# A fixed order of instructions, opposite phases of two batch halves and a shorter state update in an attention-GRU recurrence

## The chip, the cores and the metric

The kernel runs on one core of one Trainium2 chip. The metric is device time in microseconds (us) of one execution, the median of several. The profile of a run is the hardware profiler's record of one of these executions; the profile of the kernel before that the prediction was read from is of a further one. All numbers below are of that core, and all times that are compared are of runs in the fast state. (e14 and e15 ran once each, so their state is unknown; of them only the traces are compared, step by step.)

The runs fell on several chips, and this turned out to matter. The kernel before takes 2136 to 2138 us on chips 2 and 13, and 2112 to 2113 us on chips 3 and 14. I call the first kind *late* and the second *steady*, for a reason that the experiments show. Every run was timed beside runs of the kernel before on its own chip.

## The reference, cut to what matters

1024 users with 100 history items of 128 numbers go through a GRU. Its states are the keys of an attention, and also the inputs of a second recurrence, AUGRU, whose state at each user's own last step feeds a small prediction network:

```python
def augru_step(h, inp):
    x_t, a_t = inp                                   # key, attention weight of the step
    ti = jnp.concatenate([h, x_t], axis=-1)
    r = jax.nn.sigmoid(ti @ aug_Wr.T + aug_br)
    u = jax.nn.sigmoid(ti @ aug_Wu.T + aug_bu)
    h_hat = jnp.tanh(jnp.concatenate([h * r, x_t], axis=-1) @ aug_Wh.T + aug_bh)
    u = a_t[:, None] * u
    h_new = (1.0 - u) * h + u * h_hat
    return (h_new, h_new)
# ... 100 steps, state 128 wide, float32
comb = jnp.concatenate([user, item, hist_sum, item * hist_sum, attention_feature], axis=1)
scores = mlp(comb, 3 layers, sigmoid)[:, 0]          # "prediction"
```

## The kernel before

The kernel does GRU, attention and AUGRU one after the other; the GRU part is the same before and after. For AUGRU the users are sorted by length, so that a step needs only the columns of users that are still alive: a half (512 users) starts 512 columns wide and shrinks to 96. State and gates are tiles of 128 partitions by that width. Each gate is two matmuls into one PSUM bank: one on the key, which *opens* it, and one on the state, which *closes* it.

```python
ps = tile_pool(name="ps3", bufs=6, space=PSUM)      # gates
pa = tile_pool(name="pa3", bufs=2, space=PSUM)      # all else, tag "a"
...
def load_key(t, i):                                  # key of step t, half i
    k = wp.tile([P, HB], F32, name="k3", bufs=6)
    if q < WHOLE:                                    # steps 0 to 7: TensorE transposes
        ...
    else:                                            # later: VectorE, in blocks of 32
        nc.vector.transpose(k..., r[:, :w, ts(n, R)])

def step(t, i):
    ...
    pr = gate(wr, h, "pr")
    nc.scalar.activation(pr, pr, AF.Sigmoid, bias=later["br"])
    nc.vector.tensor_mul(r, h, pr)
    pu = gate(wu, h, "pu")
    nc.scalar.activation(pu, pu, AF.Sigmoid, bias=later["bu"])
    nc.vector.tensor_mul(u, pu, at)
    later["pace"] = u[:, 0:1]
    ph = gate(wh, r, "ph")
    nc.scalar.activation(ph, ph, AF.Tanh, bias=later["bh"])
    nc.vector.tensor_sub(ph, ph, h)
    nc.vector.tensor_mul(ph, u, ph)
    nc.vector.tensor_add(h, h, ph)

def predict(g, i):                                   # 128 users whose last step is past
    gather(part, part_d, g, i)                       # indirect DMA, issued by GpSimd
    ...                                              # 14 matmul passes, 4 sigmoids
    nc.gpsimd.indirect_dma_start(out=out..., in_=y)

for t in range(T):                                   # rows of keys: gathered ahead,
    for i in range(NH):                              # in blocks of 8 steps, by GpSimd
        load_att(t + 2, i)
        step(t, i)
        ... next(ahead, None)                        # some row gathers of the next block
        load_key(t + 1, i)
    for g in range(GH):
        if left <= g * P < widths[t]:
            for i in range(NH):
                predict(g, i)
```

In AUGRU the order on TensorE and ScalarE is written only for the preparations up to step 1; in the steps a scheduler orders the instructions of every engine. The row gathers are paced: each waits for a one-column copy of a fresh update weight.

## Time and profile before

| | before |
|---|---|
| median time, three runs | 2137.28 us (2135.11 to 2139.23) |
| span of the profiled execution | 2109.6 us |
| time of that execution itself | 2111.61 us |
| TensorE busy, whole span | 97% |
| AUGRU steps 2 to 99 in the profile | 604.9 us |

A page gives busy time of each engine, then 40 slices of the span in tenths, then the granted TensorE clock in tenths. A timeline line has start, length, engine, source line, operation, written and read tiles, and in brackets how long the engine had idled and what ended it. "PEld" is TensorE's weight load. The lines that carry the argument stand in the prediction.

One row of the table deserved more attention than I gave it: the profiled execution was 25.7 us faster than the median of the timed ones.

### The profile page before, as it was taken

How to read it: one execution, taken by the hardware profiler on the slowest of the kernel's cores; microseconds unless marked ns; L12 is line 12 of the kernel's file. 1: busy time of each engine (PE TensorE's matmuls, PEld its weight loads, DVE VectorE, ACT ScalarE, POOL GpSimd, SP SyncE). 2: the span in 40 equal slices, each digit the busy share in tenths (PEclk: the TensorE clock that was granted, in tenths of full speed). 3: DMA queues.
4: the chain of work that ended last, by engine and by line, in shares of the span. 5: the costliest groups of instructions: out<-in, count | busy, mean ns of one | idle time of the engine just before them, and what ended most of it. 6: DMA issues, size and time to landing. Idle time of an engine off the chain costs nothing. (4 is left out here: it accounts for less than half of the span.)

```text
span 2109.6 us, 26501 instructions
## 1 busy us (share of the span) xinstructions
PE 2046.8 (97%) x8260; PEld 979.0 (46%) x8260; DVE 1767.4 (84%) x3025; ACT 827.9 (39%) x1510; POOL 1293.4 (61%) x1295
## 2 busy tenths in 40 slices
PE   8999999999999999999999999996999999999987
PEld 3343333333333333333333333333444555688886
DVE  6888999989989888989898888996677777888765
ACT  3334343433334343334333434332443444454444
POOL 0234939479887969595969494996733443343321
PEclk9999999999999999999999999998999999999998
DMA  4533233333323343333423332213633333333221
GB/s 118 113 92 101 87 101 109 109 95 96 96 88 93 113 121 110 94 109 109 141 87 100 101 101 87 91 46 87 190 88 90 108 99 90 95 96 88 75 56 26
DMA packets 253553, 205.58 MB, mean 97 GB/s; under 512 B 74790, under 2 KB 215818, under 8 KB 253402
## 3 DMA queue, kind: packets, MB, share of 16 engines
q1 hardware_dynamic: 241082, 171.36, 29.2%
q0 software_dynamic: 12320, 32.44, 5.3%
q8 instruction: 67, 1.10, 0.2%
q14 instruction: 84, 0.69, 0.1%
HBM read 147.68 MB, written 54.40 MB: 96 GB/s over the span
## 5 line engine op out<-in xcount | busy, mean ns | idle before, releaser
L483 PE MATMUL ps<-x,wih 128*128 128x512 f32 x1200 | 591.7, 602 | 4.2 <-DMA x<-in_hist_x 4.2
L483 PE MATMUL ps<-hn,whh 128*128 128x512 f32 x1188 | 574.4, 592 | 0.0
L483 PEld LDWEIGHTS ps<-x,wih 128*128 128x128 f32 x1200 | 220.6, 190 | 327.1 <-issue 254.3
L483 PEld LDWEIGHTS ps<-hn,whh 128*128 128x128 f32 x1188 | 225.7, 190 | 284.1 <-issue 275.5
L469 POOL TENSOR_TENSOR xm<-x,m 128x512 f32<-128x512 f32 x200 | 244.8, 1224 | 128.9 <-DMA m<-mask_d 128.6
L514 ACT ACTIVATE ps<-ps,bih 128x512 f32<-128x512 f32 x200 | 132.4, 662 | 473.9 <-DVE ps L513 473.9
L495 ACT ACTIVATE r<-ps,brz 128x512 f32<-128x512 f32 x200 | 137.4, 687 | 391.3 <-PE ps L483 390.3
L470 POOL TENSOR_TENSOR hist<-hist,xm 128x512 f32<-128x512 f32 x200 | 265.9, 1330 | 15.7
L573 POOL TENSOR_TENSOR pooled<-pooled,kw 128x512 f32<-128x512 f32 x190 | 255.7, 1346 | 14.9
L572 POOL TENSOR_TENSOR kw<-kt,e 128x512 f32<-128x512 f32 x190 | 220.3, 1159 | 64.1 <-DVE e L728 64.0
L157 POOL DMA_INDIRECT rows<-keys_d,idx_k x208 | 200.0, 961 | 78.8 <-POOL rows L156 48.3
L552 DVE TENSOR_TENSOR kq<-hn,item 128x512 f32<-128x512 f32 x200 | 228.1, 1179 | 0.0
L631 PE MATMUL pm<-hn,wk 128*32 128x512 f32 x1200 | 214.1, 600 | 6.2 <-DVE f L665 3.7
L631 PE MATMUL pm<-kq,wkq 128*32 128x512 f32 x1200 | 210.9, 594 | 0.0
L631 PE MATMUL pm<-mv,w 128*32 128x512 f32 (+1 forms) x808 | 198.8, 603 | 1.4 <-ACT mv L670 0.9
L156 POOL COPY rows<-u 128x1 f32<-128x1 f32 x202 | 32.4, 181 | 259.1 <-DVE u L972 258.3
L665 DVE TENSOR_TENSOR f<-pm,q 128x512 f32<-128x512 f32 x200 | 128.3, 683 | 54.3 <-PE pm L631 54.2
L518 DVE TENSOR_TENSOR d<-hn,ps 128x512 f32<-128x512 f32 x198 | 136.0, 687 | 34.9 <-ACT ps L514 32.6
L519 DVE TENSOR_TENSOR d<-ps,d 128x512 f32<-128x512 f32 x200 | 138.3, 692 | 23.8 <-ACT ps L515 7.2
L513 DVE TENSOR_TENSOR ps<-ps,u 128x512 f32<-128x512 f32 x200 | 140.0, 700 | 21.6 <-PE ps L483 0.5
L503 DVE SCALAR_TENSOR_TENSOR u<-ps,bhh,r 128x512 f32<-128x512 f32 x198 | 146.9, 742 | 13.2 <-PE ps L483 12.9
L967 ACT ACTIVATE pr<-pr,br 128x96 f32<-128x96 f32 (+42 forms) x198 | 91.6, 463 | 136.5 <-PE pr L962 133.7
(163 smaller groups left out, 2969.9 us busy)
## 6 DMA issues: line engine op xcount, KB each, us to landing
x<-in_hist_x SPq DMA_DIRECT2D x212, 256.0 KB
keys_d<-kt SPq DMA_DIRECT2D x46, 1024.0 KB
m<-mask_d SPq DMA_DIRECT2D x200, 128.0 KB
keys_d<-kt SPq DMA_DIRECT2D x64, 64.0 KB
rows<-keys_d,idx_k POOLq DMA_INDIRECT x208, 2.8
s_b<-mv SPq DMA_DIRECT2D x200, 8.0 KB
mask_i<-in_mask SPq DMA_DIRECT2D x8, 200.0 KB
at<-att_d SPq DMA_DIRECT2D x32, 48.0 KB
```

Of the source, the lines that this page charges most:

```text
L157: nc.gpsimd.indirect_dma_start(out=r[:, k, :], out_offset=None, in_=keys_d[q], in_offset=bass.IndirectOffsetOnAxis(ap=idx_k[:, k, i : i + ...
L469: nc.gpsimd.tensor_mul(d, x, m)
L470: nc.gpsimd.tensor_add(acc, acc, d)
L483: nc.tensor.matmul(p, lhsT=w[:, g, :], rhs=v, start=(j == 0), stop=(j == len(parts) - 1),)
L495: nc.scalar.activation(r, pr, AF.Sigmoid, bias=brz[:, 0:1])
L503: nc.vector.scalar_tensor_tensor(out=u, in0=ph, scalar=bhh[:, 2:3], in1=r, op0=ALU.add, op1=ALU.mult,)
L513: nc.vector.tensor_add(pi, pi, u)
L519: nc.vector.tensor_mul(d, pz, d)
L552: nc.vector.tensor_mul(kq, h, item[:, self.cols])
L572: eng.tensor_mul(d, k, w)
L573: eng.tensor_add(acc, acc, d)
L631: nc.tensor.matmul(p[i][s, :], lhsT=w[:, s], rhs=v, start=start, stop=stop)
```

## The change

The intent: every AUGRU instruction stands in a written order on every engine, in which half 0 and half 1 work in opposite phase, so that TensorE closes a gate of one half while the other half is on ScalarE and VectorE. The state update h + u(c - h) becomes uc - (u - 1)h with (u - 1)h computed ahead of the tanh. Gates get a ring of seven banks, all else gets one. The prediction is cut into pieces that are issued one per half-step. The preparations before step 2 are reordered as well (the attention weights are gathered before the first keys are transposed), and a half-step opens the candidate (`ph`) before the update gate (`pu`).

```diff
-        ps = pools.enter_context(tc.tile_pool(name="ps3", bufs=6, space=PSUM))
-        pa = pools.enter_context(tc.tile_pool(name="pa3", bufs=2, space=PSUM))
+        ps = pools.enter_context(tc.tile_pool(name="ps3", bufs=7, space=PSUM))
+        pa = pools.enter_context(tc.tile_pool(name="pa3", bufs=1, space=PSUM))
 ...  (sort_weights, half 1 between the instructions of half 0's step 1)
             first = pa.tile([P, HB], F32, tag="a", name="first")
 ...
-        def step(t, i):
 ...  (shown above)
+        def half_step(t, i):
+            w, h = widths[t], h3[i][:, : widths[t]]
+            before, after = ((t - 1, 1), (t, 1)) if i == 0 else ((t, 0), (t + 1, 0))
+            if before in resets:
+                open_state(*before)                  # closes ph of the other half, tanh
+            pr = close_gate(t, i, "pr", wr, h)
+            pu = close_gate(t, i, "pu", wu, h)
+            nc.scalar.activation(pr, pr, AF.Sigmoid, bias=later["br"])
+            nc.scalar.activation(pu, pu, AF.Sigmoid, bias=later["bu"])
+            state = states.pop(1 - i, None)
+            if state is not None:
+                nc.vector.tensor_mul(state[0], state[0], state[1])       # u c
+            r = wp.tile([P, HB], F32, name="r3")[:, :w]
+            nc.vector.tensor_mul(r, h, pr)
+            if state is not None:
+                nc.vector.tensor_sub(state[3], state[0], state[2])       # h of the other half
+            if t == 1 and i == 0:
+                sort_weights(1, sorted_rows[1], gates[1])
+            nc.vector.tensor_mul(pu, pu, att.pop((t, i))[:, :w])
+            rest = wp.tile([P, HB], F32, name="rest")[:, :w]
+            nc.vector.scalar_tensor_tensor(                              # (u - 1) h
+                out=rest, in0=pu, scalar=1.0, in1=h, op0=ALU.subtract, op1=ALU.mult
+            )
+            later["pace"] = rest[:, 0:1]
+            resets[t, i] = r, pu, rest
+            if after[0] < T and (*after, "pr") not in opened:
+                open_gates(*after)
+            if t + 2 < T:
+                load_att(t + 2, i)
+            if t + 1 < T:
+                load_key(t + 1, i)
 ...
-        def predict(g, i):
+        def predict(g, i, pool, tag):
             gather(part, part_d, g, i)
+            yield
 ...  (a yield after each group of matmuls and of activations)
         def spread(q):
+            ahead = 2 if widths[FIRST[q]] > HB // 2 else 3
-            slots = NH * ((FIRST[q] - FIRST[q - 1] if q > 2 else FIRST[q]) - 2)
+            slots = NH * (FIRST[q] - (FIRST[q - 1] if q > 2 else 1) - ahead)
 ...
             for i in range(NH):
+                half_step(t, i)
                 for _ in range(due.pop(0) if due else 0):
                     next(ahead, None)                # row gathers
+                if jobs:
+                    try:
+                        next(jobs[0])                # one piece of a prediction
+                    except StopIteration:
+                        jobs.pop(0)
+            for g in range(1, GH):
                 if left <= g * P < widths[t]:
+                    jobs += [predict(g, i, pa, "a") for i in range(NH)]
 ...
-        with ExitStack() as pools:
+        with ExitStack() as pools, tc.manual_schedule():
             augru_phase(pools, widths)
```

More of the change, by code (lines that the diff above doesn't have):

```diff
@@ L879, in augru_phase, with bank @@
         kp = pools.enter_context(tc.tile_pool(name="kp3", bufs=4))
-        ps = pools.enter_context(tc.tile_pool(name="ps3", bufs=6, space=PSUM))
-        pa = pools.enter_context(tc.tile_pool(name="pa3", bufs=2, space=PSUM))
+        ps = pools.enter_context(tc.tile_pool(name="ps3", bufs=7, space=PSUM))
+        pa = pools.enter_context(tc.tile_pool(name="pa3", bufs=1, space=PSUM))
         wr, wu, wh = later["wr"], later["wu"], later["wh"]
-        keys, att, opened = {}, {}, {}
+        keys, att, opened, resets, states = {}, {}, {}, {}, {}
         later["pace"] = None
+        def bank(name):
+            return ps.tile([P, HB], F32, tag="g", name=name)
         def first_step(i):
@@ L890, in first_step @@
             for n, f in (("u", AF.Sigmoid), ("h", AF.Tanh)):
-                p = ps.tile([P, HB], F32, tag="g", name=f"p{n}")
+                p = bank(f"p{n}")
                 nc.tensor.matmul(p, lhsT=later["w" + n][:, 1, :], rhs=k, start=True, stop=True)
@@ L896, in first_step, with gather_weights, sort_weights @@
             return gates
-        def sort_weights(i):
+        def gather_weights(i):
             r = wp.tile([P, GH, P], F32, name="att_r", bufs=2)
-            p = pa.tile([P, HB], F32, tag="a", name="pw")
             for g in range(GH):
                 gather(r[:, g, :], pooled_d, g, i)
+            return r
+        def sort_weights(i, r, gates):
+            p = bank("pw") if i else pa.tile([P, HB], F32, tag="a", name="pw")
+            for g in range(GH):
                 nc.tensor.transpose(p[:, ts(g, P)], r[:, g, :], ident)
@@ L916, in sort_weights @@
             )
-            nc.scalar.copy(h3[i], first)
+            u, h = gates
+            nc.vector.tensor_mul(first, first, u)
+            nc.vector.tensor_mul(h3[i], first, h)
+            for t in (1, 2):
+                load_att(t, i)
         def load_att(t, i):
@@ L930, in load_key @@
             w, n, r = widths[t], t - FIRST[q], rows[q, i]
-            k = wp.tile([P, HB], F32, name="k3", bufs=6)
+            k = wp.tile([P, HB], F32, name="k3", bufs=4)
             if q < WHOLE:
-                pool, tag = (ps, "g") if t < 2 else (pa, "a")
-                p = pool.tile([P, HB], F32, tag=tag, name="pk3")
+                p = bank("pk3") if t < 2 else pa.tile([P, HB], F32, tag="a", name="pk3")
                 for g in range(-(-w // P)):
@@ L947, in open_gates, with close_gate @@
             k = keys.pop((t, i))[:, : widths[t]]
-            for m, name in ((wr, "pr"), (wu, "pu"), (wh, "ph")):
-                p = opened[t, i, name] = ps.tile([P, HB], F32, tag="g", name=name)[:, : widths[t]]
+            for m, name in ((wr, "pr"), (wh, "ph"), (wu, "pu")):
+                p = opened[t, i, name] = bank(name)[:, : widths[t]]
                 nc.tensor.matmul(p, lhsT=m[:, 1, :], rhs=k, start=True, stop=False)
-        def step(t, i):
-            w = widths[t]
-            at, h = att.pop((t, i))[:, :w], h3[i][:, :w]
-            k = keys.pop((t, i))[:, :w] if (t, i) in keys else None
-            def gate(m, v, name):
-                p = opened.pop((t, i, name), None)
-                if p is None:
-                    p = ps.tile([P, HB], F32, tag="g", name=name)[:, :w]
-                    nc.tensor.matmul(p, lhsT=m[:, 1, :], rhs=k, start=True, stop=False)
-                nc.tensor.matmul(p, lhsT=m[:, 0, :], rhs=v, start=False, stop=True)
-                return p
-            pr = gate(wr, h, "pr")
+        def close_gate(t, i, name, m, v):
+            p = opened.pop((t, i, name))
+            nc.tensor.matmul(p, lhsT=m[:, 0, :], rhs=v, start=False, stop=True)
+            return p
@@ new lines, in open_state @@
+        def open_state(t, i):
+            r, u, rest = resets.pop((t, i))
+            ph = close_gate(t, i, "ph", wh, r)
+            c = wp.tile([P, HB], F32, name="c3")[:, : widths[t]]
+            nc.scalar.activation(c, ph, AF.Tanh, bias=later["bh"])
+            states[i] = u, c, rest, h3[i][:, : widths[t]]
+        def half_step(t, i):
[10 more added lines that the diff above has]
+                nc.vector.tensor_mul(state[0], state[0], state[1])
@@ L966, in step @@
             r = wp.tile([P, HB], F32, name="r3")[:, :w]
-            nc.scalar.activation(pr, pr, AF.Sigmoid, bias=later["br"])
             nc.vector.tensor_mul(r, h, pr)
-            pu = gate(wu, h, "pu")
-            nc.scalar.activation(pu, pu, AF.Sigmoid, bias=later["bu"])
-            u = wp.tile([P, HB], F32, name="u3")[:, :w]
-            nc.vector.tensor_mul(u, pu, at)
-            later["pace"] = u[:, 0:1]
-            ph = gate(wh, r, "ph")
-            nc.scalar.activation(ph, ph, AF.Tanh, bias=later["bh"])
@@ L976, in step @@
-            nc.vector.tensor_sub(ph, ph, h)
-            nc.vector.tensor_mul(ph, u, ph)
-            nc.vector.tensor_add(h, h, ph)
-        def predict(g, i):
+            if state is not None:
[7 more added lines that the diff above has]
+            )
@@ new lines, in half_step, with last_state @@
+            later["pace"] = rest[:, 0:1]
[6 more added lines that the diff above has]
+                load_key(t + 1, i)
+        def last_state(i):
+            u, c, rest, h = states.pop(i)
+            nc.vector.tensor_mul(u, u, c)
+            nc.vector.tensor_sub(h, u, rest)
+        def predict(g, i, pool, tag):
@@ L982, in predict @@
             m0, m1 = later["m0"], later["m1"]
-            part = sp.tile([P, M0], F32, name="part3")
+            part = sp.tile([P, M0], F32, tag=f"part_{tag}", name="part3")
             gather(part, part_d, g, i)
-            f0 = sp.tile([MC, M0 // MC, P], F32, name="f0")
-            for j in range(M0 // MC):
-                p0 = pa.tile([MC, P], F32, tag="a", name="p0")
+            yield
+            n = M0 // MC
+            f0 = sp.tile([MC, n, P], F32, name="f0")
+            p0 = pool.tile([P, HB], F32, tag=tag, name="p0")[:MC, : n * P]
@@ L988, in predict @@
+            for j in range(n):
                 nc.tensor.matmul(
-                    p0, lhsT=part[:, ts(j, MC)], rhs=ident, start=True, stop=False
+                    p0[:, ts(j, P)], lhsT=part[:, ts(j, MC)], rhs=ident, start=True, stop=False
                 )
                 nc.tensor.matmul(
-                    p0,
+                    p0[:, ts(j, P)],
                     lhsT=m0[:, 4, ts(j, MC)],
@@ L997, in predict @@
                 )
+            yield
+            for j in range(n):
                 nc.scalar.activation(
-                    f0[:, j, :], p0, AF.Sigmoid, bias=later["c0"][:, j : j + 1]
+                    f0[:, j, :], p0[:, ts(j, P)], AF.Sigmoid, bias=later["c0"][:, j : j + 1]
                 )
-            p1 = pa.tile([M1, P], F32, tag="a", name="p1")
-            for j in range(M0 // MC):
+            yield
+            p1 = pool.tile([P, HB], F32, tag=tag, name="p1")[:M1, :P]
+            for j in range(n):
                 nc.tensor.matmul(
-                    p1,
-                    lhsT=m1[:, j, :],
-                    rhs=f0[:, j, :],
-                    start=(j == 0),
-                    stop=(j == M0 // MC - 1),
+                    p1, lhsT=m1[:, j, :], rhs=f0[:, j, :], start=(j == 0), stop=(j == n - 1)
                 )
+            yield
             f1 = sp.tile([M1, P], F32, name="f1")
             nc.scalar.activation(f1, p1, AF.Sigmoid, bias=later["c1"])
-            p2 = pa.tile([P, 1], F32, tag="a", name="p2")
+            yield
+            p2 = pool.tile([P, HB], F32, tag=tag, name="p2")[:, 0:1]
             nc.tensor.matmul(p2, lhsT=f1, rhs=later["m2"], start=True, stop=True)
+            yield
             y = sp.tile([P, 1], F32, name="y")
@@ L1027, in spread @@
         def spread(q):
+            ahead = 2 if widths[FIRST[q]] > HB // 2 else 3
             n = NH * -(-widths[FIRST[q]] // R)
-            slots = NH * ((FIRST[q] - FIRST[q - 1] if q > 2 else FIRST[q]) - 2)
+            slots = NH * (FIRST[q] - (FIRST[q - 1] if q > 2 else 1) - ahead)
             done = [-(-j * n // slots) for j in range(slots + 1)]
             return [b - a for a, b in zip(done, done[1:])]
-        with tc.manual_schedule(engines={mybir.EngineType.PE, mybir.EngineType.Activation}):
-            for i in range(NH):
-                load_key(0, i)
-            gates = [first_step(i) for i in range(NH)]
-            for i in range(NH):
-                load_key(1, i)
-            for i in range(NH):
-                open_gates(1, i)
-            for i in range(NH):
-                sort_weights(i)
+        sorted_rows = [gather_weights(i) for i in range(NH)]
+        for i in range(NH):
+            load_key(0, i)
+        gates = [first_step(i) for i in range(NH)]
+        for i in range(NH):
+            load_key(1, i)
+        for i in range(NH):
+            open_gates(1, i)
+        sort_weights(0, sorted_rows[0], gates[0])
         all_of(gathers(1))
         ahead, due = gathers(2), spread(2)
-        for i in range(NH):
-            load_att(1, i)
-        for t in range(T):
+        jobs, final = [], []
+        for t in range(1, T):
             if t in FIRST[2:-1]:
@@ L1054, in augru_phase @@
             for i in range(NH):
-                if t + 2 < T:
-                    load_att(t + 2, i)
-                if t:
-                    step(t, i)
-                else:
-                    pu, ph = gates[i]
-                    u = wp.tile([P, HB], F32, name="u3")
-                    nc.vector.tensor_mul(u, pu, h3[i])
-                    nc.vector.tensor_mul(h3[i], u, ph)
+                half_step(t, i)
                 for _ in range(due.pop(0) if due else 0):
                     next(ahead, None)
-                if 1 < t + 1 < T:
-                    load_key(t + 1, i)
+                if jobs:
[3 more added lines that the diff above has]
+                        jobs.pop(0)
             left = widths[t + 1] if t + 1 < T else 0
-            for g in range(GH):
+            for g in range(1, GH):
                 if left <= g * P < widths[t]:
-                    for i in range(NH):
-                        predict(g, i)
+                    jobs += [predict(g, i, pa, "a") for i in range(NH)]
+            if t == T - G:
+                final = [predict(0, i, ps, "g") for i in range(NH)]
+                for job in final:
+                    next(job)
+        open_state(T - 1, 1)
+        next(final[0])
+        last_state(1)
+        for job in jobs:
+            all_of(job)
+        next(final[0])
+        next(final[1])
+        while final:
+            for job in list(final):
+                try:
+                    next(job)
+                except StopIteration:
+                    final.remove(job)
     with ExitStack() as pools, tc.manual_schedule():
```

## The prediction

> **What bounds the kernel now.** I read the page's busy table first, then the busy slices, a table of stretches cut at the second recurrence (AUGRU), the waits inside it, and two short pieces of timeline. The page:
>
> ```profile
> PE 2046.8 (97%) x8260; PEld 979.0 (46%) x8260; DVE 1767.4 (84%) x3025; ACT 827.9 (39%) x1510; POOL 1293.4 (61%) x1295
> ...
> PE   8999999999999999999999999996999999999987
> ...
> PEclk9999999999999999999999999998999999999998
> ```
>
> TensorE (PE) is near full everywhere; it thins at slice 28, between the two recurrences, and at the end. The change touches only what comes after slice 27: AUGRU, whose first state-dependent matmul starts at 1478.6 and whose last is at 2094. Stretches (columns: stretch, its length, then busy time of PE, PEld, DVE, ACT, POOL, then granted clock, DMA share, GB/s):
>
> ```profile
> 1478.60:1919.80 441.20, 435.24 (x1440) 262.02 (x1440) 344.86 (x663) 195.63 (x366) 198.09 (x342) 1.00 0.38 105
> 1919.80:2010.60 90.80, 82.49 (x494) 76.67 (x493) 71.09 (x241) 43.44 (x124) 33.34 (x58) 0.98 0.31 82
> 2010.60:2092.50 81.90, 70.56 (x556) 66.17 (x555) 56.58 (x263) 39.24 (x138) 18.83 (x30) 0.98 0.26 46
> 2092.50:2109.60 17.10, 7.33 (x38) 5.68 (x37) 2.29 (x10) 4.33 (x14) 1.98 (x2) 0.63 0.02 5
> ```
>
> The reader is to see two regimes. A step covers both batch halves and shrinks from 512 to 96 columns. While steps are wide (to 1920, step 57) PE is busy 99%; later 86 to 91%, and no other engine is fuller. A step is 12 matmuls of 2 passes each (the trace holds 396 records for 198 matmuls of a kind), 24 passes. I timed steps by the start of the reset sigmoid of half 0. At 476 columns a step takes 9.57 us, 399 ns a pass; at 292 columns 5.89, 245 ns. Both are w/1.2 + 2 ns. Weight loads never follow each other faster than 110 ns. So PE's floor per step is 24p, with p = max(110 ns, w/1.2 + 2 ns). At 96 columns that is 2.64 us, but the step takes 3.37. This is why (one step's tail; start, length, instruction, idle before):
>
> ```profile
> 2071.97 0.32 ACT L975 ACTIVATE ph<-ph,bh 128x96 f32<-128x96 f32 x1
> ...
> 2072.32 0.27 DVE L976 TENSOR_TENSOR ph<-ph,h 128x96 f32<-128x96 f32 x1
> ...
> 2072.62 0.26 DVE L977 TENSOR_TENSOR ph<-u,ph 128x96 f32<-128x96 f32 x1
> ...
> 2072.86 0.32 ACT L975 ACTIVATE ph<-ph,bh 128x96 f32<-128x96 f32 x1 [0.58 <-PE ph L962]
> ...
> 2073.21 0.27 DVE L976 TENSOR_TENSOR ph<-ph,h 128x96 f32<-128x96 f32 x1 [0.33 <-ACT ph L975]
> 2073.38 0.24 DVE L978 TENSOR_TENSOR h<-h,ph 128x96 f32<-128x96 f32 x1
> 2073.55 0.26 DVE L977 TENSOR_TENSOR ph<-u,ph 128x96 f32<-128x96 f32 x1
> 2073.68 0.19 PEld L962 LDWEIGHTS pr<-h,wr 128*128 128x128 f32 x1 [0.57 <-DVE h L978]
> ```
>
> Half 0's last addition could start at 2072.9, but stands in VectorE's (DVE's) queue behind half 1's subtraction, which waits for its tanh. Both halves end the step together, and PE has nothing left. The other loss:
>
> ```profile
> 1945.45 0.97 POOL L157 DMA_INDIRECT rows<-keys_d,idx_k  x1 [3.09 <-issue]
> ...
> 1948.66 0.41 DVE L940 STREAM_TRANSPOSE k<-rows 128x224 f32<-128x224 f32 x1 [3.71 <-DMA rows<-keys_d,idx_k]
> ...
> 1949.92 0.30 PEld L962 LDWEIGHTS pr<-h,wr 128*128 128x128 f32 x2 [3.72 <-DVE h L978]
> ```
>
> A key transpose was placed early in DVE's queue, waits for a row gather issued late, and holds up the state behind it. The waits name this one releaser with 14.5 us in 7 waits, and long steps recur every 8 steps, where a new block of rows begins.
>
> **What the Trainium skill says.** "TensorE: Matmul & The Clock Gate", part 1, section "Wait — 56ns, not 53.3ns?" gives N/2.4 + 2.5 ns per matmul; the trace agrees if each f32 pass streams at half that rate, with 2 ns over. The same page, "LDWEIGHTS", gives 128/1.2 = 107 ns; the trace's cadence is 110. Its clock-gate section says that an idle window of about 3.4 us halves the clock: after the 3.7 us stall above, pass spacing goes from 0.17 to 0.33 us until 1953.7. And "Engine queue depths" there calls VectorE and ScalarE strict FIFOs, which is what both timelines show and what an explicit order exploits.
>
> **The change, part by part.**
> - *State algebra.* Before, tanh is followed by subtract, multiply, add: three DVE instructions. After: multiply, subtract. The other half, (u-1)h, is prepared beside the chain by a multiply and one fused instruction. DVE keeps six instructions per half-step (transpose included), so it has no less work; the end of the chain is shorter by one, about 0.27 us at 96 columns.
> - *Opposite phase.* PE now does: close candidate of half X, close reset and update of Y, open the three gates of X's next step. At 508 columns six matmuls are 5.1 us; Y's reset product is ready after about 2 matmuls + 0.27 (latency of the last pass) + 0.66 (ACT) + 0.69 (DVE) + 0.15 of hops = 3.5 us, so the next candidate never waits. Wide steps therefore sit at the floor.
> - *Narrow steps.* I follow the path that closes on itself. L = 2p + 0.27 is the time of one closing. A = 0.22 + 0.00087w is an activation (0.315 at 96, 0.66 at 508), D = 0.15 + 0.00105w a DVE instruction (0.25 at 96, 0.68 at 508); hops are 0.03 to 0.06, and independent DVE instructions start D - 0.07 apart. From the load for X's candidate: reset of Y closed at 2p + L; sigmoid and hops A + 0.06; then reset product, X's state, update weight, (u-1)h (which waits out the full D before it) and Y's key transpose; then PE opens three gates with that key, 6p, and the candidate of X's next step follows. Sum: step = 10p + 0.23 + A + 5D. At 96: 1.10 + 0.23 + 0.31 + 1.25 = 2.89 us (before 3.37). At 150: 3.39 against a floor of 3.05 (before 3.6). It crosses 24p at about 205 columns, step 62.
> - *Prefetch.* The last gather of a block is now issued two steps (wide) or three (up to 256 columns) before the block, and the transpose that needs it is the last DVE item of its half-step. With 1.3 us per gather on POOL and about 2 us to land, three steps of 4 us suffice: I book all DMA stalls as gone.
> - *7 banks.* A bank comes free within two half-steps; in the written order the seventh is what lets pu of half-step n+2 reuse a candidate bank freed at 0.8 us. No bank wait.
> - *Prediction.* Each is 14 passes, 1.55 us of PE; six in the loop remain, 9.3 us. In pieces their ACT waits are hidden.
> - *Head.* The state of half 0 is ready at 1473.4 instead of 1477.3, but PE is at half clock from 1472.4 to 1479.2, and the single "a" bank now makes the key transposes of step 2 wait for half 1's broadcast row. I count plus and minus as zero, within 2 us.
> - *Tail.* One DVE instruction less, and the last two predictions interleaved: now the second output issue is 6.9 us after the last state (2095.65 to 2102.54), my count of the pieces gives 4.5: 2.4 us.
>
> **Sum.** From step 2 to step 99 the kernel takes 2092.5 - 1487.6 = 604.9 us. After: floor of steps 2 to 56, 414.5; steps 57 to 98 by the formula, 141.6 (floor 131.9); PE key transposes 5 x 0.86 = 4.3, to which I add 0.9 for those of step 1; predictions 9.3. Together 570.6, so 34.3 less. With the tail 36.7. I give 0.7 back for semaphore instructions on DVE: 36 us less, 2137.3 - 36 = 2101.
>
> **Rivals.**
> (a) *PE alone bounds the loop* (keys ready in time, weight loads slipping ahead). Then narrow steps are 2.64 us and 9.7 us more go: 2091. For it: DVE's six starts 0.18 apart are only 1.1 us per half-step. Against: in the written order the key is transposed last, and its gates are due 6p later.
> (b) *A new wait.* Everything in program order: one late transfer on POOL (a piece that waits for its output, a pace copy) or a DVE wait stops all behind it. At 200 columns 14 gathers x 1.3 = 18 us go into five steps of 4 us, nearly full. If half of the old 14.5 us of DMA waits return: 2108; with the clock dips they bring, 2112.
> (c) *The chain is not shortened* because multiply waits behind DVE work: narrow steps stay near 3.2 us at 96: about 2107.
> (d) *The scheduler's order was already good*, because wide steps were at the floor: true for the wide part, where only 7 us can be had (432.2 against 425). This is why the change is small beside the total.
>
> **Range and chances.** All of AUGRU's excess over PE's floor is worth about 46 us, 2091. A gain over 2% needs 42.7 us, 2094.5: nearly all of it, so 0.17. Losing it would need over 20 times what the head can cost: slower 0.01. Rivals (a) and (b) give the range, 2092 to 2112.
>
> **What would show it.** Steps of 24p to about 230 columns, without the long ones every eighth step; at 96 columns 2.9 us a step, with the opening gates of the next step waiting for the key transpose; waits of a transpose on row gathers gone; clock full to the tail; second output issue about 4.5 us after the last state. Wrong if 96-column steps are at 2.65 (rival a) or above 3.1 (c), or PE gaps over 1 us with a DMA as releaser (b).

## The result, and the profile after

The kernel after took 2112.77 us (2109.92 to 2115.91, four runs), the kernel before 2138.26 us (2135.11 to 2140.40, four runs). The ratio is 0.9882, 95% interval 0.9862 to 0.9902: within 2%, as expected, but 12 us above the predicted time and 0.8 us above the top of the range. A ratio here is the mean time of one kernel's fast runs over that of the other's of the same rounds, so not quite the ratio of the medians that I quote.

The page of the profile after, busy time of each engine, and the granted clock:

```profile
PE 2049.9 (97%) x8260; PEld 985.6 (47%) x8260; DVE 1760.0 (83%) x3025; ACT 826.8 (39%) x1508; POOL 1301.5 (62%) x1301
...
PEclk9999999999999999999999999998999999999998
```

The reader sees almost the page of before, and a span of 2110.0 us where before had 2109.6: the two profiles together show no gain at all. The four stretches of AUGRU, cut at the same steps as before (columns as in the prediction: stretch, length, busy of PE, PEld, DVE, ACT, POOL, clock, DMA share, GB/s):

```profile
1474.60:1930.73 456.13, 445.78 (x1446) 271.99 (x1447) 337.43 (x661) 196.81 (x362) 206.22 (x347) 0.97 0.37 103
1930.73:2012.20 81.47, 79.91 (x488) 73.76 (x486) 70.84 (x240) 42.65 (x123) 35.58 (x60) 1.00 0.37 91
2012.20:2092.90 80.70, 72.37 (x559) 68.52 (x557) 57.14 (x265) 38.97 (x142) 19.73 (x31) 0.96 0.25 50
2092.90:2110.00 17.10, 5.70 (x44) 4.85 (x42) 2.64 (x12) 3.98 (x15) 1.98 (x2) 0.76 0.03 6
```

The middle stretch (230 down to 128 columns) gained 9.3 us and has TensorE busy 98%. The wide stretch, which I had called at its floor, is 15 us *longer*, at a mean clock of 0.97; 9.2 us of that are in step 1 (16.66 us for 7.47). The narrow one gained only 1.2 us, at 0.96. The tail is unchanged to the digit.

The single steps say which parts of the prediction held. Undisturbed wide steps are at the floor (476 columns: 9.57 us before, 9.55 after). An undisturbed step of 96 columns takes 2.88 us, against a predicted 2.89 and 3.37 before. One half-step of it, timeline of after:

```profile
2085.40 0.34 ACT L972 ACTIVATE c<-ph,bh 128x96 f32<-128x96 f32 x1 [0.57 <-PE ph L964]
...
2085.77 0.27 DVE L988 TENSOR_TENSOR pu<-pu,c 128x96 f32<-128x96 f32 x1
...
2085.97 0.25 DVE L990 TENSOR_TENSOR r<-h,pr 128x96 f32<-128x96 f32 x1
2086.01 0.39 PE L960 MATMUL ph<-k,wh 128*128 128x96 f32 x2
2086.14 0.25 DVE L992 TENSOR_TENSOR h<-pu,rest 128x96 f32<-128x96 f32 x1
```

After the tanh VectorE does uc, the other half's reset product, then the state, with nothing of the other half to wait for; before, the state stood behind the other half's subtraction. And TensorE runs key matmuls meanwhile.

But a few steps are several us too long: 27 (14.80 us, its neighbour 26 7.82), 52 (12.21), 77 (5.60), 81 (10.42). Step 27, timeline of after:

```profile
1730.34 0.95 POOL L133 DMA_INDIRECT part<-part_d,idx  x1 [0.31 <-issue]
...
1734.29 0.41 PEld L1025 LDWEIGHTS p<-ident,part 128*100 128x100 f32 x2 [4.40 <-issue]
1734.32 0.72 PE L1025 MATMUL p<-ident,part 128*100 128x128 f32 x2 [3.82 <-DMA part<-part_d,idx]
...
1737.64 0.58 ACT L972 ACTIVATE c<-ph,bh 128x384 f32<-128x384 f32 x1 [8.40 <-PE ph L964]
```

The first piece of a prediction gathers its user's rows (`part`); the next piece, one half-step later, is a matmul on them. GpSimd has row gathers to issue first, so the gather goes out at 1730.34; the data is there 4 us later; and TensorE, which must take its matmuls in the written order, stands still with the gates behind them ready to go. The skill's "TensorE: Matmul & The Clock Gate" says under "What overlaps and what doesn't" (section "The mechanism" of part 3) that matmuls start and end in program order without reordering; this trace agrees, since the closing matmul of `ph` came only after the 8 prediction passes, and ScalarE idled 8.40 us for it. The waits of after put it down to that transfer:

```profile
PE p L1025 <- DMA part<-part_d,idx: 13.8, 4, 4.9
PEld p L1025 <- DMA part<-part_d,idx: 10.8, 3, 5.1
...
PEld pr L960 <- DVE k L950: 6.1, 17, 1.3
```

(Total us, times, longest us; the first two overlap.) The third line is the wait that the prediction put on the narrow path, the next opening on the key transpose. No wait of a transpose on row gathers is left in that list, where before it was 14.5 us.

### The profile page after: what moved, and what is told of

Read it like the earlier page. It is cut to its first block, busy times and chain, and to the rows that moved or that the text cites. A ratio compares the mean times of both kernels' runs of the same rounds, so it can differ in the third digit from the quotient of the medians.

```text
span 2110.0 us, 26649 instructions
## 1 busy us (share of the span) xinstructions
PE 2049.9 (97%) x8260; PEld 985.6 (47%) x8260; DVE 1760.0 (83%) x3025; ACT 826.8 (39%) x1508; POOL 1301.5 (62%) x1301
## 5 line engine op out<-in xcount | busy, mean ns | idle before, releaser
L972 ACT ACTIVATE c<-ph,bh 128x96 f32<-128x96 f32 (+42 forms) x198 | 96.7, 488 | 277.8 <-PE ph L964 245.9
L988 DVE TENSOR_TENSOR pu<-pu,c 128x96 f32<-128x96 f32 (+42 forms) x197 | 88.9, 451 | 120.4 <-ACT c L972 107.2
L156 POOL COPY rows<-rest 128x1 f32<-128x1 f32 x208 | 39.1, 188 | 232.2 <-DVE rest L998 225.6
```

## The experiments

All results were correct unless said otherwise. "Loop" is the time from the start of half 0's reset sigmoid in step 2 to that in step 99, read from the trace. What comes before I call the head, what comes after the tail.

| run | chip | this, us | before on that chip, us | ratio, 95% interval | step 2 at | loop |
|---|---|---|---|---|---|---|
| after (the result) | late kind | 2112.77 | 2138.26 | 0.9882 (0.9862 to 0.9902) | 1493.5 | 599.4 |
| e1 before again | 2, late | 2137.21 | 2137.89 | 0.9998 (0.9989 to 1.0007) | 1504.4 | 611.9 |
| e2 part early | 2, late | 2094.13 | 2137.89 | 0.9794 (0.9775 to 0.9814) | 1496.6 | 580.7 |
| e3 own bank | 2, late | 2109.16 | 2137.89 | 0.9870 (0.9847 to 0.9892) | 1495.3 | 595.8 |
| e4 both | 2, late | 2095.67 | 2137.89 | 0.9810 (0.9793 to 0.9826) | 1495.9 | 577.6 |
| e5 key first | 3, steady | 2071.64 | 2112.96 | 0.9800 (0.9784 to 0.9817) | 1491.1 | 562.7 |
| e6 old state | 3, steady | 2091.51 | 2112.96 | 0.9896 (0.9880 to 0.9913) | 1490.5 | 582.0 |
| e7 6 banks | 3, steady | 2095.38 | 2112.96 | 0.9915 (0.9898 to 0.9931) | 1490.1 | 585.7 |
| e8 late rows | 3, steady | 2078.96 | 2112.96 | 0.9841 (0.9825 to 0.9858) | 1487.3 | 570.4 |
| e9 after again | 14, steady | 2103.14 | 2111.83 | 0.9954 (0.9937 to 0.9970) | 1492.5 | 593.5 |
| e10 both again | 14, steady | 2079.06 | 2111.83 | 0.9841 (0.9825 to 0.9858) | 1490.1 | 570.2 |
| e11 copies | 14, steady | 2082.54 | 2111.83 | 0.9856 (0.9839 to 0.9872) | 1494.1 | 570.4 |
| e12 key first again | 14, steady | 2071.37 | 2111.83 | 0.9803 (0.9787 to 0.9819) | 1489.0 | 562.7 |
| e13 tail apart | 13, late | 2083.56 | 2135.78 | 0.9759 (0.9741 to 0.9778) | 1493.4 | 571.9 |
| e14 copies again | 13, late | 2090.65 (one run) | 2135.78 | not timed | 1494.4 | 577.0 |
| e15 both, third time | 13, late | 2089.59 (one run) | 2135.78 | not timed | 1493.5 | 576.3 |

The recorded profile of before has step 2 at 1487.6 and a loop of 604.9 us.

### The part gather and the head

**e1, the kernel before unchanged.** A control, and a second profile.

> The kernel before, unchanged, profiled again. Its trace on record has a span of 2109.6 us while its timed runs take 2138 us; the changed kernel has a span of 2110.0 us and timed runs of 2113 us. Theory A: the recorded trace is an unusually good execution, and the typical one loses about 26 us more in the second recurrence, where key transposes placed early by the scheduler wait for row gathers: then this profile has a span near 2136 us, a first reset sigmoid near 1480 us as before, more than 604.9 us from step 2 to step 99 (about 631), and more than 14.5 us of transposes waiting for row gathers. Rival B: the recorded trace came from a chip on which everything is as here, and 26 us lie outside the span: then the span is near 2110 us and step 2 to 99 near 605 us. Rival C: the extra time lies in the first recurrence: then the first reset sigmoid comes near 1506 us.

The ratio was 0.9998, as a control should give. The profile was the surprise: its span is 2133.3 us, 23.7 us over the recorded one, of the same program. ScalarE's timeline at the start of AUGRU, first in the recorded profile of before, then in e1:

```profile
1482.74 0.66 ACT L975 ACTIVATE ph<-ph,bh 128x512 f32<-128x512 f32 x1 [0.22 <-PE ph L962]
1483.66 0.66 ACT L970 ACTIVATE pu<-pu,bu 128x512 f32<-128x512 f32 x1 [0.26 <-PE pu L962]
1484.52 0.66 ACT L975 ACTIVATE ph<-ph,bh 128x512 f32<-128x512 f32 x1 [0.20 <-PE ph L962]
```

```profile
1486.05 0.66 ACT L975 ACTIVATE ph<-ph,bh 128x512 f32<-128x512 f32 x1 [3.38 <-PE pk L936]
1490.36 0.66 ACT L970 ACTIVATE pu<-pu,bu 128x512 f32<-128x512 f32 x1 [3.65 <-remote]
1494.56 0.66 ACT L975 ACTIVATE ph<-ph,bh 128x512 f32<-128x512 f32 x1 [3.53 <-PE pr L962]
```

The same three activations, each after 0.2 us in one and after 3.4 to 3.7 us in the other, though the matmuls that they need had ended as promptly. The releasers named in the second fence are not tiles that these activations read, and one is called "remote": the profile does not know what ended the wait. I call this a *late start*. Step 1 takes 7.47 us in the recorded profile and 24.13 us in e1 (16.7 us more), and the loop 7.0 us more; together that is the 23.7. After the three activations shown, e1's next copy of keys (1502.92) starts 7.7 us late as well. None of the three readings foresaw this: the span is that of theory A, but the loop grew by 7.0 us and not by 26, and transposes wait for row gathers no longer than before (14.0 us, 14.5 in the recorded profile).

**e2, part early.** The gathers of both halves are issued when their group ends, and the matmuls on them at least four half-steps later.

```diff
-                    jobs += [predict(g, i, pa, "a") for i in range(NH)]
+                    new = [predict(g, i, pa, "a", 0 if i else 4) for i in range(NH)]
+                    if not jobs:
+                        for job in new:
+                            next(job)                # the gather alone
+                    jobs += new
 ...  (predict waits `lead` more pieces after its gather)
```

> The changed kernel with both part gathers of a prediction group issued as soon as the group ends, and four half-steps more between gather and first matmul. Theory: four stalls of TensorE on the part gather (4.4, 4.6, 1.1 and 5.1 us of idle before the matmul at 1734, 1905, 2016, 2033 us) and the half clock after three of them cost 17 to 20 us: expect 2094 us (2090 to 2098), steps 27, 52 and 81 within 1 us of their neighbours, no half clock in the loop. Rival: the gathers land late because the DMA queue is full of row gathers, whatever their lead, or the stall moves to a row gather behind them: then less than 6 us is gained.

It took 2094.13 us where the result had 2112.77: 18.6 us, within the expectation. Steps 27 and 28, in after (the step up to the stall, then the stretch in which the clock was lowered) and in e2 (both steps at once), columns as before:

```profile
1724.10:1733.10 9.00, 6.40 (x20) 3.42 (x19) 6.21 (x12) 2.80 (x5) 6.42 (x11) 1.00 0.43 125
1733.10:1740.00 6.90, 5.68 (x15) 3.92 (x16) 1.07 (x3) 1.13 (x2) 0.97 (x1) 0.51 0.13 38
```

```profile
1727.24:1742.57 15.33, 15.33 (x49) 9.12 (x48) 11.98 (x24) 6.55 (x12) 10.80 (x18) 1.00 0.47 125
```

TensorE waits 4 us, and then works at a clock of 0.51 for the rest of 6.9 us; so the wait costs more than its length. In e2 it is busy throughout at full clock. The list of waits of e2 has no line in which TensorE waits for `part`. Step 52 missed its expectation: it took 8.23 us beside neighbours of 5.26 and 6.46, with a late start of 2.8 us in it and 3.4 us at half clock from 1902.2.

**e3, own bank.** In after, the broadcast row of half 1 (`first`) takes the only bank of tag "a", which the key transposes of step 2 also need.

```diff
-            first = pa.tile([P, HB], F32, tag="a", name="first")
+            first = bank("first") if i else pa.tile([P, HB], F32, tag="a", name="first")
```

> The changed kernel with the broadcast row of half 1 in a bank of the ring of 7, so that the key transposes of step 2 find the single bank free. Theory: the bank wait (3.1 us of idle at 1483.7 us) and the clock it keeps halved to 1487.4 us cost 4 to 6 us: expect 2108 us (2106 to 2110), reset sigmoid of step 2 at 1488 us instead of 1493.5. Rival: the head is bound by the gathered weights and the half clock alone, not by the bank: less than 1.5 us.

It took 2109.16 us: 3.6 us less by the medians, 2.6 by the ratios (0.0012 of 2138). Neither is clear of the noise: the runs lie between 2105.64 and 2113.47 us, those of the result between 2109.92 and 2115.91, and the intervals of the ratios overlap. The weight load of the key transposes in step 2, after and then e3:

```profile
1483.65 0.71 PEld L946 LDWEIGHTS pk<-ident,rows 128*128 128x128 f32 x4 [3.09 <-issue]
```

```profile
1479.62 0.14 PEld L946 LDWEIGHTS pk<-ident,rows 128*128 128x128 f32 x1 [0.24 <-issue]
```

The wait of 3.1 us for the bank is gone. But the head of this trace has three late starts (4.3, 3.6 and 0.8 us) where that of after has none, so step 2, expected at 1488, comes at 1495.3, and on this chip what the bank is worth can't be told.

**e4, both** edits of e2 and e3.

> Both edits. If the two causes are separate the gains add: 2089 us (2085 to 2093), span from step 2 to 99 about 579 us, within 9 us of the predicted 570.6. If they are not: no more than the larger of the two, 2094 us.

2095.67 us: nothing beyond e2 (2094.13; the runs of the two overlap). Both traces have late starts in the head, of 7.8 us in e2 and 8.6 in e4. On chip 14 (e9 and e10, below) the two edits together are worth 24 us.

### Two kinds of chip

The next four runs fell on chip 3, where the kernel before took 2112.96 us, as much as the *recorded profile's own execution* (2111.61). I counted late starts as activations beginning over 0.4 us past both their closing matmul's end and ScalarE's previous work. Over the gate activations (the key copies left out) the recorded profile has none, e1 10.4 us in the head and 5.1 in the loop, after none and 4.9, e2 7.8 and 10.7, e4 8.6 and 10.1. None of the runs on chips 3 and 14 has any. So I repeated the main pair on the next call.

The packed traces tell more than the views shown here, and it shifts the blame. An activation waits for a semaphore, a counter that TensorE raises when a matmul ends. In the recorded profile TensorE's counter is raised some 14 ns after the matmul's recorded end, and a waiting activation typically starts 23 or 24 ns after that. In 73 of the 77 late starts of all late traces a raise of TensorE's counter likewise stands 20 to 85 ns before the late activation. So ScalarE seems to answer as promptly as ever, and what comes late is a signal of TensorE (of which matmul can't be told, since records are missing). The kinds of chip differ in one more thing: every late trace lacks 6 to 7% of the records of this counter (e1 has 2329 for 2478 instructions that raise it), and no steady one, nor the recorded profile, lacks any. Every timed run on record has a span and a clock, so all were recorded in some way; whether the recording itself causes the delays is an untested rival.

**e9, the kernel after unchanged.**

> The changed kernel again. The kernel before takes 2138 us on the chip of the result and of e1 to e4, and 2113 us on the chip of e5 to e8, where no activation starts late. In e1 activations start 3 to 8 us after their matmul closed, with nothing in the profile to wait for, 17 us in the head and 5 in the loop; in the changed kernel they cost about 7 us, all in the loop; in the trace on record of the kernel before none. Theory: the late starts belong to the chip and not to the kernels. On a chip like the first: before 2138, this 2113 us. On one like the second: before 2113, this 2102 us (2097 to 2106), that is, the change is worth 11 us and not 25, the part gather stalls unchanged at 17 to 20 us. Rival: the change is worth 25 us anywhere: 2088 us on the second chip.

It fell on chip 14, of the steady kind, and took 2103.14 us, the 2102 of the theory and not the rival's 2088. There the change is worth 8.7 us (0.9954), not 25.

**e10, both edits again.**

> e4 again, beside e9 on one chip. First chip: 2095 us. Second chip: theory, as in e8, which differs only in the spread of the gathers: 2079 us (2076 to 2082), step 2 to 99 at 570 us, the predicted 570.6. Gain over e9 by the part gathers and the bank: 17 us on the first, 20 to 24 us on the second. Rival: the two-step prefetch is needed after all and e8 was lucky: more than 3 us below e8.

2079.06 us. Against e9: 24.1 us by the two edits. Summed over all steps, e9 exceeds the step lengths of the prediction's formulas by 33.1 us and e10 by 9.8, so the part gathers cost 23.3 us in the loop here; those 9.8 are what the prediction had booked for the predictions' own work on TensorE (9.3).

**e11 and e14, 32 more copies.** The late starts might be bound to places in ScalarE's instruction stream. 32 one-column copies ahead of the recurrence (on e4) shift every later instruction of ScalarE against the work.

```diff
+        mark = sp.tile([P, 1], F32, name="mark")
+        for _ in range(32):
+            nc.scalar.copy(mark, ident[:, 0:1])
         gates = [first_step(i) for i in range(NH)]
```

> e4 with 32 copies of one column on ScalarE in the idle time before the first step. It tells of the late starts, if the chip has them. In e2 and e4 they stand at the same steps (28, 52, 57, 60, 66, 77, 93). Theory P: they hang on a place in ScalarE's instruction stream: 32 instructions at 6 a step move them about 5 steps earlier. Theory S: they hang on the step, that is on what else happens then: they stay. On a chip without late starts: same time as e10 within 3 us, and nothing learnt.

e11 fell on chip 14, where there are no late starts to move: it tells nothing beyond the price of the copies (3.5 us). I ran it again, with a partner:

> Version of both mends with 32 extra one-column ScalarE copies ahead of the recurrence. If this chip has late ScalarE starts (next run shows it): theory, they are bound to places in ScalarE's instruction stream, and come some 8 steps earlier than in the next run; rival, they are bound to time or to the work, and stay at the same steps. If the chip has none, the run tells nothing.

> Partner of the run with extra copies: on a chip with late ScalarE starts, late starts at steps 28, 52, 57, 60, 66, 77, 93 as before and some 10 us in the loop; on the other chip none.

Both fell on chip 13, which has late starts. In the loop of e15 they stand in steps 53, 66, 67, 77 and 93; in e14 in the same and in 57: at the same work, not 32 instructions earlier. So in the loop they are not bound to a place in ScalarE's instruction stream. Nor to a time: step 93 has one in after and in e2, e3, e4, e13, e14 and e15, at times from 2050 to 2076 us. In the head e15 has two (1.6 and 2.2 us) and a key copy 2.9 us late, and e14 has none. What they hang on stays open.

### What the parts of the change are worth, on steady chips

e5 to e8 ran side by side on chip 3. Their partner with both edits alone, e10, ran on chip 14; e8, which took the same time as e10, ties the two chips together.

**e8, late rows** (on e4): row gathers spread up to one step before their block, not two or three.

```diff
-            ahead = 2 if widths[FIRST[q]] > HB // 2 else 3
-            slots = NH * (FIRST[q] - (FIRST[q - 1] if q > 2 else 1) - ahead)
+            slots = NH * (FIRST[q] - (FIRST[q - 1] if q > 2 else 1) - 1)
```

> e4 with the row gathers of a block spread up to one step before the step that transposes its first key, instead of two or three steps. Theory: the eleven block starts wait again for row gathers: 0.5 to 1.5 us each in wide steps, 2 to 3 us in narrow ones, some 12 us in all, 2107 us, and transposes waiting for row gathers appear among the waits. Rival: written order alone removed those waits (the transpose sits at the end of its half-step, not ahead): within 3 us of 2095.7 us.

2078.96 us against 2079.06 for e10; loop 570.4 against 570.2. No transpose waits for rows. The earlier issue that I had given the credit to isn't needed. That it is enough for the transpose to stand last in its half-step is my reading of this; no run moves the transpose alone with late rows.

**e7, six banks** (on e2): gates 6, the rest 2, as before.

```diff
-        ps = pools.enter_context(tc.tile_pool(name="ps3", bufs=7, space=PSUM))
-        pa = pools.enter_context(tc.tile_pool(name="pa3", bufs=1, space=PSUM))
+        ps = pools.enter_context(tc.tile_pool(name="ps3", bufs=6, space=PSUM))
+        pa = pools.enter_context(tc.tile_pool(name="pa3", bufs=2, space=PSUM))
```

> e2 with 6 banks in the ring and 2 beside it, as in the kernel before. Theory: the opening of an update gate then reuses the bank of the update gate two half-steps back, which is free only when that half's state is done, near the end of the half-step; the path is 2(4p + L + 0.12 + A + 2D - 0.07): 3.57 us a step at 96 columns (2.88 in e2), 4.1 at 148, 5.8 at 256 (5.3 in e2), unchanged above 400; about 40 us more, 2135 us. Rival, as the name of the change may be read: the seventh bank is a reserve that is not needed: within 4 us of e2's 2094 us.

2095.38 us, 16 us over e10; a 96-column step takes 3.34 us instead of 2.88 (I had worked out 3.57, and 40 us in all: too much). Weight loads of e7 in such a step:

```profile
2062.51 0.30 PEld L960 LDWEIGHTS ph<-k,wh 128*128 128x128 f32 x2
2063.01 0.30 PEld L960 LDWEIGHTS pu<-k,wu 128*128 128x128 f32 x2 [0.20 <-DVE r L990]
```

With six banks the opening of `pu` needs the bank that VectorE's reset product is still reading: 0.50 us between two loads that otherwise are 0.22 apart, in both half-steps. At 256 columns and more nothing is lost (5.15 us, the floor).

**e6, old state** (on e4): subtract, multiply, add after the tanh again.

```diff
-                nc.vector.tensor_mul(state[0], state[0], state[1])
+                nc.vector.tensor_sub(state[1], state[1], state[3])
+                nc.vector.tensor_mul(state[1], state[0], state[1])
             ...
-                nc.vector.tensor_sub(state[3], state[0], state[2])
+                nc.vector.tensor_add(state[3], state[3], state[1])
 ...  (and no `rest`)
```

> e4 with the state update of the kernel before (subtract, multiply, add after tanh; no (u-1)h beside the chain), all else as in e4. Theory: the reset product then starts behind two dependent DVE instructions, its path is 2(L + 0.17 + A + 3D - 0.07): 3.29 us a step at 96 columns (2.88 in e4), 3.8 at 148 (3.37), 4.4 at 200 (4.12), nothing in wide steps; some 15 us more in all, 2110 us. Rival: DVE has as many instructions as before, so the algebra buys nothing in opposite phase: 2096 us, 2.9 us a step.

2091.51 us, 12.5 us over e10. At 96 columns 3.28 us a step against 2.88, at 148 columns 3.82 against 3.39: the expected sizes.

**e5 and e12, key first** (on e4): the key transpose stands ahead of the update weight on VectorE, because in after the next opening waits for it.

```diff
+            if FIRST[WHOLE] <= t + 1 < T:
+                load_key(t + 1, i)
             nc.vector.tensor_mul(pu, pu, att.pop((t, i))[:, :w])
             ...
-            if t + 1 < T:
+            if t + 1 < FIRST[WHOLE]:
                 load_key(t + 1, i)
```

> e4 with the key transpose of a half-step ahead of the update weight and of (u-1)h on VectorE (from step 8 on). It tests the path that the prediction put under narrow steps, 10p + 0.23 + A + 5D, which runs through three DVE starts before the transpose. Theory: with the transpose earlier the next path bounds, 2(4p + 0.39 + A + D), candidate closed, reset closed, sigmoid, product: 2.77 us a step at 96 columns (2.88 in e4), 3.1 at 148 (3.37 in e4), wide steps unchanged; 5 to 6 us off the sum, 2090 us. Rival: the key is not on the path, narrow steps stay at 2.88 and the time at 2095.7 us.

> e5 again, beside e9 and e10 on one chip, as the version that beats both kernels. Second chip: 2071.6 us, 6 to 8 us under e10, by 5.7 us in narrow steps. First chip: 2089 us (2085 to 2093).

2071.64 us on chip 3 and 2071.37 on chip 14, on the latter 7.7 us less than e10, a little more than the 5 to 6 expected. With the step of 2.77 us this confirms that in after the narrow steps hang on the key transpose. VectorE's timeline in e5 at 96 columns:

```profile
2042.01 0.27 DVE L950 STREAM_TRANSPOSE k<-rows 128x96 f32<-128x96 f32 x1
2042.20 0.23 DVE L997 TENSOR_TENSOR pu<-pu,at 128x96 f32<-128x96 f32 x1
2042.47 0.26 DVE L1000 SCALAR_TENSOR_TENSOR rest<-pu,h 128x96 f32<-128x96 f32 x1
```

A 96-column step takes 2.77 us, as expected. This is the best version that is correct: 41 us below the kernel before on the same chip (0.980, with an interval on both sides of 2%).

### The tail

**e13, tail apart** (on e5): half 1's last output rows go to a scratch tensor, so that the two last transfers write different tensors. The result is wrong on purpose in those 128 rows (they stay unwritten, and the error comes out as not a number).

```diff
-                out=out.rearrange("(b o) -> b o", o=1),
+                out=(spare_out if (g, i) == (0, 1) else out).rearrange("(b o) -> b o", o=1),
```

> The key-first version, but half 1's last output row goes to a scratch tensor in device memory instead of the output (wrong on purpose in those 128 rows). Theory: in the tail GpSimd holds the second output transfer for 3.2 us because the first one, into the same tensor, has not landed; then the second issue comes about 4.5 us or less after the last state instead of 6.7, and the span ends 1.5 to 3 us earlier, 2069 on the steadier chip. Rival: the second issue waits for y or for GpSimd's own work; then nothing moves, 2071.

The end of the timeline in after, and then in e13:

```profile
2099.35 1.00 POOL L1055 DMA_INDIRECT out<-y,idx  x1 [24.45 <-ACT y L1054]
2099.40 0.26 ACT L1054 ACTIVATE y<-p,c 128x1 f32<-128x1 f32 x1 [0.33 <-PE p L1051]
2103.08 0.98 POOL L1055 DMA_INDIRECT out<-y,idx  x1 [2.73 <-issue]
```

```profile
2072.16 1.00 POOL L1061 DMA_INDIRECT out<-y,idx  x1 [21.83 <-ACT y L1060]
2072.21 0.26 ACT L1060 ACTIVATE y<-p,c 128x1 f32<-128x1 f32 x1 [0.33 <-PE p L1057]
2073.47 0.99 POOL L1061 DMA_INDIRECT spare_out<-y,idx  x1 [0.30 <-issue]
```

In both, half 1's result `y` is ready 0.3 us after the first issue. In after GpSimd holds the second issue until 3.7 us after the first; with another target it goes out after 1.3 us. So the second transfer waited for the first, which writes the same tensor. From the last state (ready at 2069.22) to the second issue it is 4.25 us, where the prediction counted 4.5; from the last state to the end of the span 11.0 us, against 13.9 in e12 (chip 14). The total of 2083.56 us says nothing of it: the run fell on a late chip, on which the key-first version was not timed.

## Why the prediction was right or wrong

The path by which the time was wrong is best followed on the steady chips, since the trace that it was read from is of that kind. There the change should have given 36 us; it gave 8.7 (traces of before and e9: 5.9).

- **Wide floor, narrow formula: right.** 2.88 us for 2.89 at 96 columns, 3.39 for 3.39 at 148 to 150, 9.55 for 9.57 at 476. Rivals (a) and (c) fall: steps were neither 2.65 nor above 3.1. (Two readings of the prediction are a little off, without weight: by the formula the narrow regime begins at about 211 columns and not at 205, and the 110 ns hold for the gates' weight loads, while smaller ones of the prediction network follow each other at 68 to 90 ns.) Once nothing else disturbs, the loop is 570.2 to 570.4 us (e10, e8) for a predicted 570.6. The algebra is worth 12.5 us of this (e6) and the seventh bank 16 (e7).
- **"I book all DMA stalls as gone": the step that failed.** It was true of the row gathers, and for another reason than the one given (e8). But I looked only for the stalls of before. The change itself makes a new one: "in pieces their ACT waits are hidden" looked at ScalarE and not at the first piece, a gather of 4 us with a half-step of 1.5 to 4 us to hide it. Rival (b), "one late transfer on POOL ... stops all behind it", named the mechanism and gave a price, 2112 with the clock dips; I put it at the edge of the range. That the price fits is luck: it counted row gathers, of which none waits. It cost 18.6 us (e2), 23.3 of the loop on a steady chip.
- **"I count plus and minus as zero": wrong by about 5 us.** In e9 step 2 comes at 1492.5 and in the recorded profile of before at 1487.6. I had seen the bank that makes the key transposes wait; with a bank of its own step 2 comes at 1487.3 to 1491.1 on the steady chips (e8 and e5; e10: 1490.1), so part of the 5 us may be the bank's, but one trace of e9 against a spread of 3.8 us doesn't show how much. The clock doesn't settle it: the half clock of the head lasted 6.8 us in before, 13.7 in e9, and with the bank of its own from 3.4 (e8) to 13.7 (e5). The cause of this part stays open.
- **Tail, 4.5 us: the count was right, the wait was missed.** The pieces do take 4.25 us (e13), but the second output waits for the first, and the issue came 6.7 us after the last state. The gain of 2.4 us became nothing.
- **The sum on the steady chips.** Of 34.3 us in the loop 11.4 came (604.9 - 593.5): 22.9 short. Head 4.9 lost. Tail 2.9 short (17.1 us after step 99 before, 17.6 in e9, for a predicted 14.7). The 0.7 given back as a margin wasn't needed. 36 - 22.9 - 4.9 - 2.9 + 0.7 = 6.0, against 5.9 in the traces.
- **"2137.3 - 36": the base was of another kind of chip.** The trace had a time of 2111.6 us and I subtracted its gain from 2137.3. The 25.7 us between them stood in the record, unasked. They are late starts and what follows from them (23.7 us in e1), and they also changed with the kernel: the traces of before and after on late chips differ by 23.3 us (2133.3 - 2110.0), of which the steady chips show 5.9. The remaining 17.4 are mostly late starts in the head: before has 16.7 us of delay in step 1 (24.13 us for 7.47), while the step 1 of after takes 16.7 us on both kinds of chip (result and e9). This is one trace of each; e2, with the same head as after, has a step 1 of 20.76 us, so the new head isn't free of them. So the 2112.77 that was measured is close to the predicted 2101 for partly the wrong reasons: about 30 us of gain lost against the prediction's sum, and 17 found that it had not known of.

What stays open is the cause of the late starts. They come on some chips and not on others; they are not bound to a place in ScalarE's instruction stream (e14). They often stand in the same steps, and it is a signal of TensorE that comes late, not ScalarE's answer to it.

## What to carry to other kernels

An explicit order takes away the scheduler's freedom to step round a late transfer, so when work is cut into pieces and put in a fixed order, every piece that begins with a transfer needs its own count: when is it issued behind what else, when does it land, and what stands behind its first user. A wait of TensorE can cost more than its length: in after the waits of 3.8, 4.2 and 4.9 us on a gather were each followed by 3.4 to 6.8 us at half clock, and in e9 one of only 1.7 us was (2012.2), while in after one of 0.9 us was not. And before a gain read from a trace is subtracted from a time, the time of the traced execution itself should be held against it.

## What the Trainium skill lacked or had wrong

- "TensorE: Matmul & The Clock Gate", "HAM oscillation": in its example the clock stays low for about 1.67 us after a wait; here one wait of about 4 us on a gather brought 6.9 us at a clock of 0.51 (1733.1 to 1740.0), and the head of e9, with several shorter waits, had 13.7 us on end. Its section "What's actually happening" has the window of about 3.4 us, and the lengths seen here are two and four of those.
- The same page gives N/2.4 + 2.5 ns per matmul in its section "Wait — 56ns, not 53.3ns?" for bf16. That section has no figure for float32; here a matmul is two passes of w/1.2 + 2 ns each (9.55 us for a step of 24 passes at 476 columns).
- "DMA: Bandwidth & Descriptors", "Anatomy of one DMA — SWDGE (gpsimd) path", has about 2.0 us of fixed cost per transfer, most of it the write receipt. The indirect gather here took 3.95 us from the start of its issue (1730.34) to the first weight load on its data (1734.29), 0.95 us of it GpSimd's own instruction. An output scatter that has to wait for another to the same tensor was issued 3.7 us after it, against 1.3 us with a tensor of its own.
- No page tells that two chips can run one program 24 us apart (2136 to 2138 us against 2112 to 2113) in the same state, by instructions that start up to 7.7 us after their visible inputs are ready, with the signal that they wait for recorded just before them.
